# An attention block with a convolution for its queries: the first dense stage in another order, and the cast of later queries one slot later

## The chip, the core and the metric

The kernel runs on one core of a Trainium2 chip. The metric is the time of one execution in microseconds (us) on the device. TensorE is called PE, VectorE DVE, ScalarE ACT, GpSimd POOL and SyncE SP, as in the profile.

## The reference

`x` is [4, 384, 48, 48] in float32: 4 images, 384 channels, 2304 pixels each. Per image:

```
local  = depthwise 7x7 convolution of x, scaled and shifted per channel
qkv    = layernorm(x over channels) @ qkv_w.T + qkv_b      # 8 heads of 48
q      = q + layernorm(local)                              # the convolution goes to the queries
attn   = softmax(q @ k.T * 48**-0.5)                       # 2304 x 2304 per head
out    = x + (attn @ v) @ proj_w.T + proj_b
```

## The kernel before

**Tiles.** Channels lie on the 128 partitions in three chunks. The dense stage (values, keys, queries from the normed x) goes by six groups of 384 columns (8 rows of 48 pixels). The attention goes by query tiles: 4 images x 5 tiles t of 8, 10, 10, 10 and 10 rows (384 or 480 columns). Each tile has 12 slots (four pairs of heads x three batches of keys). A slot is `score_batch` (36 matmuls, L1099; one exp on ACT per two banks, L1107) and `weigh_batch` (24 matmuls, L1114), 9.1 us of PE at 480 columns and 7.4 at 384.

**Order.** PE, DVE, ACT and SP run in the order in which the program is written (a manual schedule). POOL does so only up to `loads.close()`; from there a scheduler places its instructions. Each instruction waits on semaphores for what it reads.

**Convolution.** It runs on DVE, one instruction per tap and chunk (L337; 147 for a tile), for the next tile while PE works at this one. In the first dense stage the taps are placed by hand with `convolve_first(n)`; after that `plan()` deals them out in proportion to a table of free DVE time at each point (slots: `spare`; dense stages of later images: `spare_at_keys`, points ("kv", t, g, h)) and to the due time of each tile. What the first stage has made beyond tile 0's 147 taps is `made`, where the plan starts. Tile 1's first chunk is convolved on PE (`products`, L410).

**Norms.** The class `Norm` takes the mean over channels by a matmul with a matrix of constants. `mean_by_chunk` uses three matmuls, one for each chunk (L688, the line of `project`). `sum_squares` (two DVE adds, L560 and L561) and `mean_in_place` (one matmul, L593) do the same with DVE's adds. Then `centre` (L603), `squares` (ACT, L550), `root` (ACT, L611 to L613), `newton` (DVE, L625 and L626), `scale` (L683).

**First dense stage** (image 0, lines 1157 to 1268): group 0's x comes from the convolution's slab; weights are loaded into `staged[2]` (values), `staged[1]` (keys) and `staged[0]` (queries) and scaled by the norm's gain on ACT (L899, L906, L907). `shift_rows` (L862) and `columns` (L888) give the share of the norm's beta in the biases, which `key_bias` and `query_bias` (L910 to L916, DVE) add. `from_x` is a generator: each `next` (two in `both`) issues matmuls of values, keys or queries of a group and their evictions; `lows_out` writes the low parts of the keys (L798). `convolve_first`, the norm of the next group and these steps are interleaved by hand. SP issues, in order: the vectors, slab(0, 0) in two parts, the three weights, x of groups 1 to 5 (four DMAs each), the output weights `w_o`, and later `copies_in` (L358) for the shifted rows that `products` reads. POOL loads the slab of tile 1, which `conv_ops(0)` issues with its first tap.

**Queries.** `local_end` and `query_end` (L936, L948) make a tile's queries from the normed convolution and q. Each pair of heads is split in a high part (`high_queries`: cast on ACT, L962) and a low part (`low_queries`: subtraction on DVE, L967, and six DMAs on SP, L972 and L974, that stack rows). The scores of a pair read all of them. For the first pair of the next tile this happens in the slots of this tile: in image 0 and at t = 0 with the full norm ("early"), from t = 5 on with the short norm ("following", `few_...`, slots `first` = 5 and `second` = 8). `jobs` are ACT instructions that `weigh_batch` issues behind the exps of its slot. `query_end(t, True)` puts the cast between its first and second DVE instruction.

Of the kernel before, what the change touches and what calls it, by code (L numbers as in the profile page):

```python
# [10 lines left out]
F32 = mybir.dt.float32  # L11
# [5 lines left out]
P = 128  # L17
# [31 lines left out]
def unshifted_pass(  # L49
# [16 lines left out]
    nc = tc.nc  # L66
    B, C, N = x.shape
    W = 48
    H = N // W
    CC = C // P  # L70
    G = RG * W
    NG = N // G
# [7 lines left out]
    NT = B * NA  # L80
# [31 lines left out]
    def load_packed(dst, src, queue=nc.sync):  # L112
        for p0, piece in segments(src):
            queue.dma_start(out=dst[p0 : p0 + piece.shape[0]], in_=piece)
# [5 lines left out]
    def place_x(b, g):  # L120
        xn[b, g] = whole[:, :, g * G : (g + 1) * G]
        return xn[b, g]

    def load_x(b, g, queue=nc.gpsimd):
        load_packed(place_x(b, g), x[b, :, g * G : (g + 1) * G], queue)

    slabs = {}

    def load_slab(b, g, parts=1, queue=nc.gpsimd):
        first, end = max(0, row_of[g] - PAD), min(H, row_of[g + 1] + PAD)  # L130
        t = work.tile([P, CC, GM + 2 * PAD * W], F32, tag="slab", name=f"slab{b}_{g}")

        edges = (first, row_of[g + 1], end) if parts == 2 else (first, end)
        for a, e in zip(edges, edges[1:]):
            load_packed(t[:, :, (a - first) * W : (e - first) * W], x[b, :, a * W : e * W], queue)
        slabs[b, g] = (t, first, end)

# [58 lines left out]
                    )  # L196

    load_by_pair(of_ln, ln_pair, (nc.scalar, nc.gpsimd))
    load_slab(0, 0, 2, nc.sync)
    place_x(0, 0)  # L200
    nc.gpsimd.tensor_scalar_add(inv, norms[:, 3], BN_EPS)
    nc.gpsimd.tensor_tensor(inv, inv, neg_half, ALU.pow)
# [26 lines left out]
    def pack():  # L229
# [23 lines left out]
        work.tile([P, CC, GM], F32, tag="qs", name="copies", bufs=5).rearrange("p c n -> p (c n)")  # L253
        for _ in range(2)
    ]
    staged = [
        work.tile([P, CC, GM], F32, tag="qs", name="staged", bufs=5)[:, :, :C] for _ in range(3)
    ]
    load_packed(staged[2], qkv_wT[:, 2 * C :])
    load_packed(staged[1], qkv_wT[:, C : 2 * C])  # L260
    load_packed(staged[0], qkv_wT[:, 0:C])
    for g in range(1, NG):
        load_x(0, g, nc.sync)
    load_by_pair(qk_vec, qk_b, (nc.gpsimd, nc.gpsimd))
    with nc.allow_non_contiguous_dma(reason="a few vectors, once"):
        load_packed(vbp, v_b.rearrange("o c -> c o"), nc.gpsimd)
    nc.gpsimd.dma_start(out=pb, in_=proj_b)
    load_packed(w_o, proj_wT)
    loads.close()


# [33 lines left out]

    def conv_ops(t):
        b, g = divmod(t, NA)
        if t + 1 < NT:
            load_slab(*divmod(t + 1, NA))
        slab, first, end = slabs[b, g]  # L310
        if t == 0:
            begin_sums(0)
            begin_sums(1)
        while soon:
            soon.popleft()()
        acc = accs[t]

        order = [(tap, c) for tap in taps for c in range(CC)]
        if t == 1:
            order = [o for o in order if o[1]]  # L320
        for i, (tap, c) in enumerate(order):
            if i == len(order) - AHEAD and t + 1 < NT:
                if t:
                    begin_sums(t + 1)
                soon.append(lambda: first_taps(t + 1))
            part = window(slab, acc[:, c, :], g, first, end, c, tap)
            if not part:
                continue
            src, dst = part
            weight = cw[:, c, tap : tap + 1]  # L330
            if tap == taps[0]:
                if t == 0:
                    nc.vector.tensor_scalar(
                        dst, src, weight, shift[:, c : c + 1], ALU.mult, ALU.add
                    )
            else:
                nc.vector.scalar_tensor_tensor(dst, src, weight, dst, ALU.mult, ALU.add)  # L337
            if t == 0 or tap != taps[0]:
                yield
# [11 lines left out]
    def copies_in():  # L351

        slab, first, end = slabs[0, 1]
        slab = slab[:, 0].rearrange("p (h w) -> p h w", w=W)
        for q, rows in enumerate(quarters):
            for i, to in enumerate(quarters):
                n = min(rows_kept, end - first - i)
                nc.sync.dma_start(out=copy_of(q)[to, 0:n], in_=slab[rows, i : i + n])  # L358
# [104 lines left out]
    def spare_at_keys(b, g, h):  # L463
        time = 4.6 - {0: 0.6, 2: 0.7, 3: 1.4, 4: 1.2}.get(h, 0.0)
        if g < later(b):
            time -= {0: 2.3, 2: 2.2, 4: 2.3}.get(h, 0.0)
        if 0 < g <= later(b):
            time -= {1: 0.4, 3: 2.6}.get(h, 0.0)
        return time - {
            (1, 1): 1.0, (2, 1): 1.4, (4, 0): 2.3, (4, 2): 2.2, (4, 4): 2.3, (5, 0): 0.4,  # L470
            (5, 1): 4.5, (5, 2): 0.6, (5, 3): 1.5, (5, 4): 3.0,
        }.get((g, h), 0.0)

    points, room = [("start",)], [FIRST_ROOM]
# [278 lines left out]
    def keep_stack(b, i):  # L753
        at = slice(i * third, (i + 1) * third)
        nc.gpsimd.dma_start(out=wide[b, 0][:, :, at], in_=stacks[b, 0, i].bitcast(F32))
# [81 lines left out]
    def both(making):  # L837
        next(making)
        next(making)
        while soon:  # L840
            soon.popleft()()

    def lows_out(n):
        for _ in range(n):
            lows.popleft()()
# [72 lines left out]
    def output_bias():  # L918

        m = two_banks()[:, 0, 0:CC]  # L920
        for co in range(CC):
            project(
                m[:, co : co + 1],
                lambda c: w_o[:, c, co * P : (co + 1) * P],
                lambda c: vbp[:, c, :],
            )
        added = const.tile([P, CC], F32, tag="inv", name="added")
        nc.scalar.copy(added, m)
        return added
# [4 lines left out]
    def local_end(t, rs):  # L934
        acc = accs[t]
        nc.vector.scalar_tensor_tensor(acc, acc, -1.0, rs, ALU.mult, ALU.mult)  # L936
# [21 lines left out]
    def high_queries(t, p):  # L958
        qs = work.tile([P, 3, GM], HALF, tag="qs", name=f"qs{t}_{p}", bufs=5)
        qs = qs[:, :, : columns_of(t)]  # L960
        stacked[t, p] = qs
        nc.scalar.copy(qs[:, 0, :], query_of(t, p))  # L962
# [184 lines left out]
    def convolve_first(n):  # L1147
        nonlocal n_first
        n_first += n
        for _ in range(n):  # L1150
            next(stream)
# [28 lines left out]
    both(making)  # L1180
    shift_rows()
    rows_out()
    copies_in()
    spread_out()
    next(making)
    for c in range(CC):
# [2 lines left out]
    convolve_first(10)  # L1189
    norm = Norm(xn[0, 1])  # L1190
    norm.mean_by_chunk(norm.src, bank)
    convolve_first(18)
    key_bias(m)
    convolve_first(3)
    query_bias(m)
# [1 line left out]
    norm.centre()  # L1197
    norm.squares()
    both(making)
    convolve_first(2)  # L1200
    norm.mean_by_chunk(norm.buf)
    norm.root()
    both(making)
    convolve_first(4)
    lows_out(3)
    norm.scale(norm.newton())
    both(making)
    convolve_first(7)
    norm = Norm(xn[0, 2])
    norm.sum()  # L1210
    for g in range(1, NG):

        last = g == NG - 1
        making = from_x(0, g)
        both(making)
        if last:
            added = output_bias()
        else:
            norm.mean_in_place()
            convolve_first(6)  # L1220
        if g in (3, 5):
            keep_stack(0, g // 2 - 1)
        norm.centre()
        norm.squares()
        if last:
            convolve_first(6)
        both(making)
        if last:
            norm.mean_by_chunk(norm.buf)
        else:  # L1230
            if g == 1:
                taps_out()
            if g == 2:
                products()
                convolve_first(24)
            convolve_first(5)
            norm.sum_squares()
            both(making)
            norm.mean_in_place()
        norm.root()  # L1240
        if last:
            convolve_first(9)
            local_end(0, norm.newton())
            query_end(0, True)
            both(making)
            low_queries(0, 0, nc.scalar)
            convolve_first(2)
            lows_out(1)
            both(making)
            convolve_first(4)  # L1250
            both(making)
            continue
        lows_out(1)
        both(making)
        convolve_first(6)
        lows_out(2)
        norm.scale(norm.newton())
        both(making)
        if g == NG - 2:
            assert n_first >= each  # L1260
            norm = Norm(accs[0])
            norm.mean_by_chunk(norm.src)
        convolve_first(5)
        if g < NG - 2:
            norm = Norm(xn[0, g + 2])
            norm.sum()
    lows_out(2)
    nc.vector.tensor_add(pb, pb, added)
    made = n_first - each
# [3 lines left out]
    for t in range(NT):  # L1273
# [74 lines left out]
        for s in range(NSLOT):  # L1348
# [26 lines left out]
                norm_x.scale(norm_x.few_newton())  # L1375
            if following and s == second + 1:
                local_end(t + 1, norm.few_newton())
                query_end(t + 1, True)
            if coming and s == X_SLOTS[0] + 1:
                jobs.extend(norm_x.square_jobs())  # L1380
            if following and s == first + 1:
# [40 lines left out]
                low_queries(t, pair + 1)  # L1422
            if t and early and s == first + 1:
                norm.sum_squares()
            if following and s == second + 1:
                low_queries(t + 1, 0)
            if coming and s == X_SLOTS[0]:
                norm_x.few_centre()
# [579 lines left out]
```

## Time and profile before

| | before |
|---|---|
| runs, us | 2738.39, 2740.79, 2745.3 (median 2740.79) |
| profiled execution, us | 2736.99 |
| its span, us | 2735.1 |
| mean granted clock of PE | 0.999 |
| DVE busy, convolution alone (L337), us | 2313.1, 1657.9 |
| PE: weighing (L1114), scoring (L1099), us | 1166.2, 968.5 |
| first scores of tile 0 start at, us | 161.04 |
| scores of tile 1 start at, us | 255.66 |
| last projections start at, us | 2694 |

The span is that of the profiled execution; its time has 1.9 us around the span. In the views, a row names line, engine, operation, tile written <- tiles read, shapes and count; a bracket at its end gives the engine's idle time just before it and what ended it. A row of the timeline has the start and the length in us first, and joins several like instructions into one (x12). The view of waits lists, for an engine, the instruction that waited, what it waited for, the sum, how often and the longest, in us.

### The profile page before, as it was taken

The numbers are of one execution on the slowest core, as the hardware profiler recorded it, in microseconds if no ns is written. First come the engines' busy times: TensorE is split into PE (matmuls) and PEld (weight loads), VectorE is DVE, ScalarE is ACT, GpSimd is POOL, SyncE is SP. The second block draws the span as 40 slices with busy tenths as digits, with TensorE's granted clock in tenths as the row PEclk, the third lists the DMA queues.
The fourth block names the chain that finished last, engine by engine and source line by source line (L and its number), as shares of the span: only waits on it lengthen the run. The fifth ranks groups of instructions, "written<-read, shape, count | busy, mean of one in ns | idle before, by whom it ended". The sixth has DMA issues, their size and how long they took to land.

```text
span 2735.1 us, 46034 instructions
## 1 busy us (share of the span) xinstructions
PE 2715.1 (99%) x16442; PEld 1536.5 (56%) x16442; DVE 2313.1 (85%) x4036; ACT 1671.0 (61%) x2317; POOL 599.5 (22%) x1073
## 2 busy tenths in 40 slices
PE   8999999999999999999999999999999999999999
PEld 5565555555566555555555655555555665555555
DVE  7999999989998899988889899889788898986212
ACT  4356777777325767777622677777752377766762
POOL 4541101102452111011155210111225511110110
PEclk9999999999999999999999999999999999999999
DMA  8354535446456545354555553545536545444442
GB/s 164 85 153 129 143 112 138 126 128 179 107 146 162 133 124 147 112 156 117 150 138 135 166 152 104 143 127 144 144 111 159 153 134 135 136 134 130 141 150 68
DMA packets 160480, 370.46 MB, mean 135 GB/s; under 512 B 58673, under 2 KB 107857, under 8 KB 160241
## 3 DMA queue, kind: packets, MB, share of 16 engines
q0 software_dynamic: 71232, 278.45, 36.1%
q1 hardware_dynamic: 83696, 78.92, 12.6%
q10 hardware_dynamic: 5312, 10.06, 1.1%
q8 instruction: 132, 2.16, 0.3%
q14 instruction: 108, 0.88, 0.1%
HBM read 258.14 MB, written 64.14 MB: 118 GB/s over the span
## 4 chain that ended last, share of the span: by engine, by line
PE 89%; DVE 8%; DMA 2%; ACT 1%; SPq 0%; issue 0%; POOL 0%; DVEq 0%; ACTq 0%
PE o L1114 37%; PE r L1099 31%; PE r L688 20%; DVE acc L337 6%; DMA xn<-in_x_dram 1%; DMA rd<-den 0%; PE r L410 0%; DMA qs<-qs 0%; DMA slab<-in_x_dram 0%; SPq L974 0%; DVE acc L936 0%; DVE xn L948 0%; DMA staged<-in_qkv_wT_dram 0%; PE r L587 0%; DVE ao L1010 0%
## 5 line engine op out<-in xcount | busy, mean ns | idle before, releaser
L337 DVE SCALAR_TENSOR_TENSOR acc<-slab,vec,acc 128x470 f32<-128x470 f32 (+10 forms) x2832 | 1657.9, 656 | 4.2 <-ACT acc L300 4.2
L1107 ACT ACTIVATE pt<-r 128x960 f32<-128x960 f32 (+1 forms) x1440 | 1248.5, 943 | 246.1 <-PE o L1114 151.0
L1114 PE MATMUL o<-pt,v 128*64 128x480 f32 (+1 forms) x5760 | 1166.2, 554 | 0.4 <-ACT pt L1107 0.4
L1099 PE MATMUL r<-qs,ks 64*128 64x480 f32 (+1 forms) x8640 | 968.5, 373 | 3.1 <-DMA qs<-qs 1.2
L1099 PEld LDWEIGHTS r<-qs,ks 64*128 64x128 f32 x8640 | 785.0, 184 | 268.1 <-issue 173.2
L1114 PEld LDWEIGHTS o<-pt,v 128*64 128x64 f32 x5760 | 392.7, 137 | 659.7 <-issue 566.7
L760 POOL DMA_DIRECT2D ks<-wide x220 | 159.6, 726 | 1350.6 <-PE r L1099 1282.4
L688 PE MATMUL r<-xn,w_qk 128*128 128x384 f32 x864 | 284.2, 486 | 0.0
L991 ACT COPY o<-o 113x480 f32<-113x480 f32 (+1 forms) x160 | 87.1, 544 | 279.0 <-PE o L1114 278.5
L688 PEld LDWEIGHTS r<-xn,w_qk 128*128 128x128 f32 x864 | 164.1, 190 | 114.6 <-issue 0.7
L688 PE MATMUL r<-w_v,xn 128*128 128x384 f32 x432 | 146.9, 492 | 2.8 <-ACT w_v L899 2.5
L782 ACT COPY v<-r 128x384 f32<-128x384 f32 x72 | 32.1, 481 | 186.5 <-PE r L688 186.5
L1010 DVE TENSOR_TENSOR ao<-ao,o 113x480 f32<-113x480 f32 (+1 forms) x120 | 75.7, 631 | 71.6 <-ACT o L991 71.6
L688 PEld LDWEIGHTS r<-w_v,xn 128*128 128x128 f32 x432 | 82.2, 192 | 62.8 <-issue 4.1
L745 POOL DMA_DIRECT2D wide<-k x144 | 72.0, 502 | 100.4 <-ACT k L795 76.5
L967 DVE TENSOR_TENSOR qs<-xn,qs 128x480 fp32r<-128x480 f32 (+1 forms) x60 | 37.9, 632 | 60.1 <-ACT qs L962 60.1
L688 PE MATMUL r<-af,w_o 128*128 128x384 f32 (+1 forms) x270 | 85.2, 470 | 0.0
L1010 DVE TENSOR_TENSOR aot<-aot,o 113x480 f32<-113x480 f32 (+1 forms) x40 | 25.3, 632 | 62.7 <-ACT o L991 62.6
L1001 ACT COPY ao<-o 113x480 f32<-113x480 f32 (+1 forms) x60 | 32.6, 543 | 68.7 <-PE o L1114 68.7
L795 ACT ACTIVATE k<-r,qkb 128x384 fp32r<-128x384 f32 x72 | 39.3, 580 | 53.5 <-PE r L688 39.1
L812 ACT ACTIVATE xn<-r,qkb 128x384 f32<-128x384 f32 x72 | 39.9, 577 | 51.3 <-PE r L688 50.1
L1080 DVE SCALAR_TENSOR_TENSOR xr<-r,pb,xr 128x384 f32<-128x384 f32 (+2 forms) x72 | 41.9, 611 | 34.0 <-PE r L688 25.2
(147 smaller groups left out, 1358.6 us busy)
## 6 DMA issues: line engine op xcount, KB each, us to landing
ks<-wide POOLq DMA_DIRECT2D x220, 768.0 KB, 5.1
qs<-qs SPq DMA_DIRECT2D x352, 60.0 KB
slab<-in_x_dram POOLq DMA_DIRECT2D x24, 432.0 KB, 7.1
wide<-k POOLq DMA_DIRECT2D x96, 96.0 KB, 2.2
wide<-ks POOLq DMA_DIRECT2D x12, 768.0 KB, 4.9
xr<-in_x_dram POOLq DMA_DIRECT2D x16, 576.0 KB, 5.8
rb<-rden SPq DMA_DIRECT2D x32, 270.0 KB
held<-ao POOLq DMA_DIRECT2D x12, 720.0 KB, 3.9
```

Of the source, the lines that this page charges most:

```text
L337: nc.vector.scalar_tensor_tensor(dst, src, weight, dst, ALU.mult, ALU.add)
L688: nc.tensor.matmul(dst, lhsT=weights(c), rhs=src(c), start=c == 0, stop=c == CC - 1)
L745: nc.gpsimd.dma_start(out=last[16 * u : 16 * u + 16, 0], in_=k[r : r + 16, 0])
L760: queue.dma_start(out=place_keys(b, p, i), in_=wide[b, p][:, :, at])
L795: nc.scalar.activation(k[:, 0, :], r[:, :G], AF.Identity, bias=bias)
L812: nc.scalar.activation(src[:, i, :], q[:, :G], AF.Identity, bias=qkb[:, 0, i : i + 1])
L991: nc.scalar.copy(part[0 : 64 + HA], sums[0 : 64 + HA, 0, :n])
L1010: nc.vector.tensor_add(dst, dst, part[0 : 64 + HA])
L1080: nc.vector.scalar_tensor_tensor(xr[:, co, :], m, pb[:, co : co + 1], xr[:, co, :], ALU.add, ALU.add)
L1099: nc.tensor.matmul(r[:, j, :n], lhsT=ks[rows, w, at], rhs=qs[rows, m, :], start=i == 0, stop=i == 2,)
L1107: nc.scalar.activation(pt, r[:, :, :n], AF.Exp, scale=SCALE)
L1114: nc.tensor.matmul(sums[halves[j], 0, : columns_of(t)], lhsT=values[t // NA, kb // NB][:, first : first + 64], rhs=pt[:, j, :], start=i == ...
```

## The change

Five edits, all in the order of work; the arithmetic of the result is the same.

1. **Value weights first.** `load_slab` takes a function to call between its two parts; the DMAs of `staged[2]` go between the two parts of slab(0, 0) on SP. The staging tiles are allocated before the others.
2. **Loads.** x of group 1 is loaded alone, x of groups 2 and 3 and of 4 and 5 as pairs (8 DMAs fewer on SP). `w_o` goes from the end of SP's loads to POOL, written behind the norm's root in group 0; slab(0, 1) is written there too, and no longer in `conv_ops(0)`. `copies_in` is issued later.
3. **Key bias sooner**: 9 instead of 18 steps of `convolve_first` stand ahead of it.
4. **Chunk sums behind a norm.** The mean of squares of group 1 and of the convolution of tile 0 are taken by `sum_squares` and `mean_in_place` instead of `mean_by_chunk`. The taps of the first stage are placed anew; `made` goes from 32 to 21. The last group is written by itself behind the loop.
5. **Later casts.** For a "following" tile the cast comes as a job in slot `second + 2` = 10, `low_queries` at the end of slot 10 instead of 9; `query_end` no longer holds the cast. Two entries of the table `spare_at_keys` change.

```diff
-    def load_slab(b, g, parts=1, queue=nc.gpsimd):
+    def load_slab(b, g, parts=1, queue=nc.gpsimd, between=None):
...
         for a, e in zip(edges, edges[1:]):
+            if a != first and between is not None:
+                between()
...
-    load_slab(0, 0, 2, nc.sync)
+    load_slab(0, 0, 2, nc.sync, lambda: load_packed(staged[2], qkv_wT[:, 2 * C :]))
...
-    load_packed(staged[2], qkv_wT[:, 2 * C :])
     load_packed(staged[1], qkv_wT[:, C : 2 * C])
     load_packed(staged[0], qkv_wT[:, 0:C])
-    for g in range(1, NG):
-        load_x(0, g, nc.sync)
+    load_x(0, 1, nc.sync)
+    for g in range(2, NG, 2):
+        place_x(0, g)
+        place_x(0, g + 1)
+        at = slice(g * G, (g + 2) * G)
+        load_packed(whole[:, :, at], x[0, :, at], nc.sync)
...
-    load_packed(w_o, proj_wT)
     loads.close()
...
-        if t + 1 < NT:
+        if 0 < t < NT - 1:
             load_slab(*divmod(t + 1, NA))
...
-            (5, 1): 4.5, (5, 2): 0.6, (5, 3): 1.5, (5, 4): 3.0,
+            (5, 1): 4.5, (5, 2): 0.6, (5, 4): 1.5,
...
-    convolve_first(18)
+    convolve_first(9)
     key_bias(m)
...
     both(making)
-    convolve_first(2)
-    norm.mean_by_chunk(norm.buf)
+    convolve_first(3)
+    norm.sum_squares()
+    norm.mean_in_place()
     norm.root()
+    load_slab(0, 1)
+    load_packed(w_o, proj_wT, nc.gpsimd)
     both(making)
...
+    making = from_x(0, NG - 1)
+    both(making)
+    added = output_bias()
+    keep_stack(0, 1)
+    norm.centre()
+    norm.squares()
+    convolve_first(3)
+    norm.sum_squares()
+    norm.mean_in_place()
+    norm.root()
+    both(making)
+    convolve_first(6)
+    local_end(0, norm.newton())
+    query_end(0, True)
+    both(making)
+    low_queries(0, 0, nc.scalar)
+    convolve_first(4)
+    lows_out(1)
+    both(making)
+    convolve_first(8)
+    both(making)
     lows_out(2)
...
             if following and s == second + 1:
                 local_end(t + 1, norm.few_newton())
-                query_end(t + 1, True)
+                query_end(t + 1)
+            if following and s == second + 2:
+                jobs.append(lambda: high_queries(t + 1, 0))
...
-            if following and s == second + 1:
+            if following and s == second + 2:
                 low_queries(t + 1, 0)
```

In the loop over the middle groups (1 to 4) the conv's steps move too: 8 behind `mean_in_place` (6 before), 5, 33 or 9 ahead of `sum_squares` (5, 29 and 5 before), 4 behind `lows_out(1)` (6 before), and in group 4 five steps ahead of the mean of tile 0's convolution, where they stood behind it; `norm.scale` comes ahead of `lows_out(2)`.

## The prediction

> **What bounds the kernel now.** I read the page first, then the waits of PE, then the timelines of the stretches that the diff touches. The page, busy time and chain:
>
> ```profile
> PE 2715.1 (99%) x16442; PEld 1536.5 (56%) x16442; DVE 2313.1 (85%) x4036; ACT 1671.0 (61%) x2317; POOL 599.5 (22%) x1073
> ...
> PE o L1114 37%; PE r L1099 31%; PE r L688 20%; DVE acc L337 6%; DMA xn<-in_x_dram 1%; DMA rd<-den 0%; PE r L410 0%; DMA qs<-qs 0%; DMA slab<-in_x_dram 0%; SPq L974 0%; DVE acc L936 0%; DVE xn L948 0%; DMA staged<-in_qkv_wT_dram 0%; PE r L587 0%; DVE ao L1010 0%
> ```
>
> PE is busy in 99% of 2735.1 us: the time is PE's work plus its waits. The view of PE's waits (us in total, times, longest) shows how little is left to gain:
>
> ```profile
> PE r L593 <- DVE sq L561: 2.7, 1, 2.7
> PE r L688 <- ACT w_v L899: 2.5, 2, 2.0
> PE r L688 <- ACT sq L550: 2.5, 1, 2.5
> PE r L1157 <- POOL one L166: 1.8, 1, 1.8
> PE r L1099 <- DMA qs<-qs: 1.2, 2, 0.9
> PE r L1099 <- issue: 1.1, 1, 1.1
> ```
>
> All its waits make some 15 us, the largest in the first dense stage (0 to 161 us). Taking every one away could not give 1%. A new wait at a place that recurs could cost more. So I walk the first stage, then the casts, which come twelve times.
>
> **First stage, up to the second group's norm.** PE's timeline from 14 to 42 us (start, length, what, wait before it):
>
> ```profile
> 16.26 0.91 PE L688 MATMUL r<-w_v,xn 128*128 128x384 f32 x2 [1.98 <-ACT w_v L899]
> 17.70 5.19 PE L688 MATMUL r<-w_v,xn 128*128 128x384 f32 x10 [0.53 <-ACT w_v L899]
> 22.81 2.11 PE L862 MATMUL r<-staged,of_ln 128*1 128x384 f32 x18
> ...
> 30.82 2.17 PE L688 MATMUL r<-xn,mean_w 128*128 128x384 f32 x6 [0.57 <-DMA xn<-in_x_dram]
> 32.83 4.03 PE L688 MATMUL r<-xn,w_qk 128*128 128x384 f32 x12
> 39.34 2.20 PE L688 MATMUL r<-sq,mean_w 128*128 128x384 f32 x6 [2.48 <-ACT sq L550]
> ```
>
> Value weights first take away the two waits (2.5 us). PE then meets other gates sooner: the last key and query weights (staged[1] lands at 18.5, used from 22.81) and x of group 1 (its last DMA landed at 30.70, PE waited 0.57). So this part alone buys nothing that group 1's x does not allow; call X its landing. Six value matmuls between 17.7 and 22 us took 6.0 us where 3.9 is their time at full clock: the granted clock was 0.50 from 18 to 21 us, after that idling. Whether that stretch goes or moves, it lies ahead of X.
>
> w_o, 590 KB, was last on SP, behind x. Read in the schedule of the changed kernel, its first DMA (221 KB) stands at the head of POOL's queue and the others behind slab(0,1), whose DMAs were issued at 4.3 and 15.2 to 17.4 us. It now competes with x of group 1. Before, 140 to 211 GB/s were moved in each ten us up to 40 us, with the 16 engines' share at 1.08 between 15 and 30 us: they were full. If w_o takes nothing from x, X stays at 30.7, and 28.5 is the bound if x gains too. If all 590 KB go first, at 180 GB/s that is 3.3 us: 34.0. Before, some 0.5 MB of later groups had already come by 30.7, so SP loses only part: I take 31.7, near the row.
>
> The Trainium skill speaks against this move: "Trainium Kernel Development and Optimization", section Key Constraints, says that DMAs of SP's, ACT's and POOL's queues all run on the same 16 engines and interleave, and that several queues save only the time to issue. The full share agrees; by this rule alone X would be the 34.0 above, by the row of x's landing 30.7.
>
> Key bias sooner: before, the centring of group 1 (L603) began at 36.73, behind 27 taps (0.51 us each) that kept the key bias back to 34.83. Now nine taps fewer stand ahead, so the centring C waits for X: mean 1.94 (six records of 0.32) and bias, C = X + 2.4 = 34.1. From C to the next group's mean of squares (63.17 before, "L593") three more taps (1.5) and two adds (1.06) must run on DVE; less the idle they fill this path is 28.8 instead of 26.4. So that mean moves by (C - 36.73) + 2.35: -0.3 at X = 31.7, -1.3 at 30.7, +2.0 at 34.
>
> **First stage, the rest.** Chunk sums behind a norm: a mean by chunk is three matmul instructions of 0.645 us; one remains. Two norms x 2 x 0.645 = 2.6 us less on PE. DVE gets two adds of 1.06. From that mean to the first scores took 97.87 us (63.17 to 161.04); without the second mean and a wait of 0.33 PE's own work is 95.5. But two waits come. In group 4, the mean of the conv's result now stands behind five taps: DVE is ready 7.85 after the norm's mean, PE at 6.45: 1.4. In the last group the mean follows output_bias at once, and needs a copy (0.16), squares (1.17 on ACT), the sum (1.06) and 0.14: 2.7. Sum 99.6, +1.75. The dense stage ends **1.5** later (-1.7 at 28.5, +0.5 at 30.7, +3.8 at 34). The POOL and SP moves otherwise (keep_stack, copies, eight SP DMAs fewer) lie beside PE work; the copies are used only at 78.8 us.
>
> Eleven taps fewer are done in the first stage, and the planner gives them to later slots. In tile 0 DVE had no idle time from 157 to 240 us and PE already waited 0.52 at the norm (237.12). DVE now starts 1.0 later against PE and has two taps more ahead (1.25): **+2.3** (0 to 3.3). At tiles 1 to 4 DVE idles over 5 us before each query: nothing is carried on.
>
> **Later casts.** For the 12 tiles from the fifth on that are not first of an image, `low_queries` moves from the end of slot 9 to the end of slot 10, behind slot 10's taps on DVE. Its six DMAs on SP (3.7 us to issue) must land before the next tile's first scores. The same order exists already at tile 1; DVE there, and then PE:
>
> ```profile
> 248.58 0.65 DVE L967 TENSOR_TENSOR qs<-xn,qs 128x480 fp32r<-128x480 f32 x1
> 249.15 5.47 DVE L337 SCALAR_TENSOR_TENSOR acc<-slab,vec,acc 128x450 f32<-128x450 f32 x9
> ```
> ```profile
> 255.66 0.92 PE L1099 MATMUL r<-qs,ks 64*128 64x480 f32 x5
> 257.49 1.79 PE L1099 MATMUL r<-qs,ks 64*128 64x480 f32 x14 [0.91 <-DMA qs<-qs]
> ```
>
> From the subtraction to PE going on are 8.9 us, with a wait. At tiles 2 and 3 the gap was 8.44 without a wait, at tile 4 9.85 with 0.2; a 384-column tile needed 5.4 to 6.4 (835.34 to 841). I call it the need: 5.4 to 9.85, taken as 8.0, nearest the rows of 480 columns. Now the tiles of 480 columns, DVE and PE around tile 7:
>
> ```profile
> 1024.90 4.27 DVE L337 SCALAR_TENSOR_TENSOR acc<-slab,vec,acc 128x450 f32<-128x450 f32 x7
> 1029.09 0.65 DVE L967 TENSOR_TENSOR qs<-xn,qs 128x480 fp32r<-128x480 f32 x1
> 1029.65 12.42 DVE L337 SCALAR_TENSOR_TENSOR acc<-slab,vec,acc 128x450 f32<-128x450 f32 x20
> ```
> ```profile
> 1036.62 3.79 PE L1114 MATMUL o<-pt,v 128*64 128x480 f32 x18
> 1040.34 2.85 PE L1099 MATMUL r<-qs,ks 64*128 64x480 f32 x24
> ```
>
> The slack is 1040.34 - 1029.09 = 11.25. Behind 13 taps more (0.62 each, 8.2 with what else is there) 3.05 are left, 4.95 short of the need. In the same way (slack, delay, wait): tile 6: 11.2, 6.2, 3.0; tile 8: 14.4, 7.7, 1.3; tile 11: 11.9, 6.2, 2.3; tile 16: 12.4, 5.7, 1.3; tiles 9, 12 to 14 and 17 to 19 have 17.4 to 19.7 and wait for nothing. Sum **+12.9**; 17.4 with a need of 8.9, 4.8 with 6.2, 2.8 with 5.4. In each tile DVE waits for something that PE's end of the tile before sets (rd, L1036), so one wait does not pay for the next.
>
> What the later cast gives: ACT no longer stands before an exp waiting for the query:
>
> ```profile
> 1022.58 0.59 ACT L962 CAST qs<-xn 128x480 fp32r<-128x480 f32 x1 [3.39 <-DVE xn L948]
> ```
>
> There PE's scores took 5.07 instead of 4.10 us: 0.97 back. But it lies in tile 6, ahead of tile 7's scores, which then come sooner by as much and wait longer: **0** net. Planner: with its table, five taps more (two at one point, three at the next; 3.2 us) stand ahead of the last residual sum (L1080 at 839.18) before tile 5 and hold its PSUM; of them some 1.3 fall into a wait that PE had there anyway (1.07 at 840.72): **+1.9** (0 to 2.4; at tiles 10 and 15 DVE idles 3.5 and 2.5 there and hides it).
>
> Sum: 1.5 + 2.3 + 12.9 + 0 + 1.9 = +18.6. Against the profiled execution (2736.99; span 2735.1) that is 2755.6. The median of the runs, 2740.79, lies 3.8 above it: **2759**.
>
> **The rivals.**
> *The DMAs land sooner* (the other side: not slower). Mechanism: at slot 11 little else is on SP, the need is the 5.4 of the 384-column tile. Place: the starts of tiles 6, 7, 8, 11, 16. Price 2.8 instead of 12.9; with X at 30.7 the sum is 0.5 + 2.3 + 2.8 + 1.9 = +7.5, 2748. It decides from a need of about 5.5 down. For it: 5.4 was seen. Against: six issues alone take 3.7 and every 480-column row is at 8.4 or above.
> *x late and the need long.* w_o's bytes all ahead of x (X = 34, +3.8) and a need of 8.9 to 9.85 (17.4 to 22): 3.8 + 2.3 + 1.9 + 20 = +28, 2769. For it: the DMA share above 1.0 up to 30 us.
> *It does what its words say.* PE loses 2.6 us of matmuls and the first waits, DVE hides the sums, and the later casts only remove ACT's block: -2 to -5, 2737. Against: DVE has no gap in 157 to 240 us, and five boundaries have under 15 us of slack.
>
> **How the numbers follow.** Forecast 0.55, sooner landing 0.20, late x 0.13, as its words say 0.12. 0.3% (8.2 us) is about what a measurement of this kernel can tell from no change. Faster needs under 2732.6: part of the last case and what no row shows, 0.10. Same: most of the second case and the rest of the last, 0.24. Slower: 0.66. The range takes in the lower bounds (-1.7 + 2.3 + 2.8 + 0, 2744) with a little of the last case, and the late x: 2741 to 2770.
>
> **What would show it.** In the changed profile: waits of L1099's successor on DMA qs<-qs at the starts of tiles 6, 7, 8, 11, 16, of 1 to 5 us; x of group 1 landing at 31 to 32 and PE's mean there; new waits before the mean near 138 and 146 us; the first scores at 162 to 163; a wait of some 2.8 at the norm near 239. I am wrong if PE has no qs waits at those boundaries, or if the first scores start before 160.

## The result and the profile after

The changed kernel takes 2770.43 us (median of 4 runs, 2768.09 to 2779.42) against 2741.28 (2738.39 to 2745.3): 1.0111 times as long, 95% interval 1.0085 to 1.0137, or 29 us more. Forecast were 18 more, 2759, and at most 2770. The profiled execution is the slowest of the four, 2779.42 us (span 2777.6), 42.4 above the profiled one of before; its mean granted clock is 0.990, that of the other three 0.993 or 0.994, of before 0.999.

The page of the changed kernel, busy time and chain:

```profile
PE 2732.5 (98%) x16434; PEld 1547.8 (56%) x16434; DVE 2317.0 (83%) x4040; ACT 1672.4 (60%) x2317; POOL 602.4 (22%) x1077
...
PE 79%; DVE 11%; DMA 5%; issue 2%; ACT 1%; SPq 0%; POOL 0%; DVEq 0%; ACTq 0%; POOLq 0%
```

PE has 8 records less to do and is busy 17 us longer: the same matmuls took more time. Its waits (total, times, longest, in us):

```profile
PE r L1103 <- DMA qs<-qs: 13.8, 7, 3.9
PE r L597 <- DVE sq L565: 7.6, 2, 5.0
PE r L692 <- DVE acc L341: 2.8, 1, 2.8
PE r L1161 <- POOL mean_w L165: 2.8, 1, 2.8
PE r L692 <- issue: 2.4, 1, 2.4
PE r L692 <- DMA xn<-in_x_dram: 2.4, 1, 2.4
```

All idle time of PE, short gaps included, is 45.1 us in place of 20.0 (span less busy time): 25.1 more, where the span grew by 42.5. The other 17.4 are PE's own busy time, and the clock makes them. PE's timeline of the first stage (start, length, wait in the bracket) shows it in the lengths:

```profile
10.54 3.80 PE L692 MATMUL r<-slab,mean_w 128*128 128x128 f32 x18 [2.37 <-issue]
...
23.95 3.94 PE L866 MATMUL r<-staged,of_ln 128*1 128x384 f32 x18 [1.97 <-DMA pb<-in_proj_b_dram]
...
35.57 4.18 PE L692 MATMUL r<-xn,mean_w 128*128 128x384 f32 x6 [2.36 <-DMA xn<-in_x_dram]
...
69.18 1.62 PE L597 MATMUL r<-sq,mean_w 128*128 128x384 f32 x2 [5.00 <-DVE sq L565]
149.05 2.97 PE L692 MATMUL r<-acc,mean_w 128*128 128x384 f32 x6 [2.82 <-DVE acc L341]
161.31 1.62 PE L597 MATMUL r<-sq,mean_w 128*128 128x384 f32 x2 [2.59 <-DVE sq L565]
```

Compare with before: the same six mean matmuls took 2.17 us there and 4.18 here, the 18 of the beta rows 2.11 and 3.94, two records of a mean 0.88 and 1.62. Each slow row stands behind a bracket of about 2 us or more. Not every such bracket has a slow row behind it. In the kernel before, this one has none:

```profile
63.17 0.88 PE L593 MATMUL r<-sq,mean_w 128*128 128x384 f32 x2 [2.68 <-DVE sq L561]
```

The granted clock gives the same: the profiled execution has 11 stretches at 0.50 while PE works, each 3.4 us long or 6.8, 51 us together; before it had one of 3.4. Half of that, less what lies in PE's idle time, is lost: PE is busy 17.4 us longer although the change takes 2.6 us of matmuls away, so the clock costs **some 20 of the 42 us** of this execution, and the waits the rest. It is the slowest of the four. By its clock (0.990, against 0.993 or 0.994 and 0.999 before), the other three lose some 12 of their 29 us in this way: an estimate in proportion, as only this execution has a trace.

Where the two profiled executions part (start of the first scores of a tile, us):

| start of | before | after | behind | half of the time at half clock so far, waits included, after |
|---|---|---|---|---|
| tile 0 | 161.04 | 178.69 | 17.7 | 15.4 |
| tile 1, second slot | 266.09 | 286.39 | 20.3 | 17.1 |
| tile 5, second slot | 848.28 | 874.10 | 25.8 | 18.8 |
| tile 6, second slot | 938.52 | 969.93 | 31.4 | 20.5 |
| tile 7 | 1040.34 | 1069.75 | 29.4 | 20.5 |
| tile 11 | 1595.11 | 1624.52 | 29.4 | 20.5 |
| tile 12 | 1704.05 | 1741.58 | 37.5 | 23.9 |
| tile 17 | 2367.73 | 2409.82 | 42.1 | 25.6 |

The first stage loses 17.7, the tiles behind it 24.4. (Before, the last column is 1.7 throughout.)

### The profile page after: what moved, and what is told of

It is laid out like the page before. It is cut to its first block, busy times and chain, and to the rows that moved or that the text cites. A ratio compares the mean times of both kernels' runs of the same rounds, so it can differ in the third digit from the quotient of the medians.

```text
span 2777.6 us, 46010 instructions
## 1 busy us (share of the span) xinstructions
PE 2732.5 (98%) x16434; PEld 1547.8 (56%) x16434; DVE 2317.0 (83%) x4040; ACT 1672.4 (60%) x2317; POOL 602.4 (22%) x1077
## 3 DMA queue, kind: packets, MB, share of 16 engines
q1 hardware_dynamic: 82352, 78.33, 12.6%
## 4 chain that ended last, share of the span: by engine, by line
PE 79%; DVE 11%; DMA 5%; issue 2%; ACT 1%; SPq 0%; POOL 0%; DVEq 0%; ACTq 0%; POOLq 0%
PE o L1118 36%; PE r L1103 30%; PE r L692 12%; DVE acc L341 7%; DMA four<-parts 1%; DMA qs<-qs 1%; DMA parts<-part 1%; DVE k L802 1%; DMA xn<-in_x_dram 1%; DMA staged<-in_qkv_wT_dram 0%; DVE xr L1084 0%; PE r L414 0%; DVE sq L565 0%; DVE xn L952 0%; DMA wide<-k 0%
## 5 line engine op out<-in xcount | busy, mean ns | idle before, releaser
L1103 PE MATMUL r<-qs,ks 64*128 64x480 f32 (+1 forms) x8640 | 976.7, 375 | 16.3 <-DMA qs<-qs 13.8
L816 ACT ACTIVATE xn<-r,qkb 128x384 f32<-128x384 f32 x72 | 40.0, 579 | 50.5 <-PE r L692 49.2
L692 PEld LDWEIGHTS r<-af,w_o 128*128 128x128 f32 x270 | 51.3, 190 | 31.9 <-DVE k L802 0.2
```

The costliest lines, as they stand in the source:

```text
L692: nc.tensor.matmul(dst, lhsT=weights(c), rhs=src(c), start=c == 0, stop=c == CC - 1)
L816: nc.scalar.activation(src[:, i, :], q[:, :G], AF.Identity, bias=qkb[:, 0, i : i + 1])
L1103: nc.tensor.matmul(r[:, j, :n], lhsT=ks[rows, w, at], rhs=qs[rows, m, :], start=i == 0, stop=i == 2,)
```

## The experiments

**Theory A**: idle stretches of PE of some 1.5 us and more are followed by stretches at half clock, so that a wait costs its length and 1.7 or 3.4 us more. (The bound did not hold as a rule: see the last section.) **Theory B**, the rival (and the way the prediction counted): a wait costs its length. Beside them stands which edit makes which wait. In brackets behind a median stand the median of the kernel before, measured beside it, the ratio and its 95% interval.

**e1: the first stage alone.** The last edit undone, table and all.

```diff
-                query_end(t + 1)
-            if following and s == second + 2:
-                jobs.append(lambda: high_queries(t + 1, 0))
+                query_end(t + 1, True)
-            if following and s == second + 2:
+            if following and s == second + 1:
                 low_queries(t + 1, 0)
```

> The changed kernel with its last edit undone: casts and low parts of the later queries where they were, and the old table of the planner. In the changed profile the tiles from 5 on lose 21.4 us (from 20.65 behind at the end of tile 4 to 42.09 behind at tile 17). Theory A (every wait of PE longer than about 1.5 us is followed by stretches of 3.4 us at half clock, so it costs its length and 1.7 to 3.4 more): all of that goes, waits and stretches at tiles 5, 6, 11, 15 and 16; against the changed kernel -17 to -22 us, some 2750. Theory B (the waits alone cost): the qs and residual waits of these tiles sum to 13.5 us, so -13 us, some 2757. If the first stage alone made the loss, nothing changes.

Measured: 2754.3 us (2740.47; 1.0045, 1.0028 to 1.0062), 16 below the changed kernel, between the two numbers: the time does not decide between the theories. In its profile no tile from 6 on loses anything; tile 5's part of the path still holds a wait of 3.0 (for an eviction on ACT, L816) and one stretch, so that loss is not the last edit's alone. So the first stage, with this wait, costs some 14 us and the casts some 16 here.

**e2: the casts alone**, the same edit in the kernel before.

> The kernel before with the last edit alone (later casts and the new table). Theory A: waits at the starts of tiles 5, 6, 11 and 16, each with a half-clock stretch behind it where it is longer than 1.5 us: +17 to +22 us, some 2760, mean clock below 0.998. Theory B (waits alone): +13, some 2754, clock as before. The prediction's own sum for this part was +14.8 with waits at tiles 6, 7, 8, 11 and 16.

Measured: 2759.49 (2740.47; 1.0064, 1.0047 to 1.0081), +19.0, and mean clock 0.994 to 0.996: theory A. (The interval's lower end is +12.9, so it is the clock more than the time that rules out B.) The new waits are at tiles 5, 6, 11 and 16, as expected; the stretches behind 5, 6 and 11 were 6.8, 3.4 and 10.2 us long. With e1 the parts sum to 14 + 19 = 33; together they made 29.

**e3: w_o back on SP.**

```diff
     nc.gpsimd.dma_start(out=pb, in_=proj_b)
+    load_packed(w_o, proj_wT)
     loads.close()
...
-    load_packed(w_o, proj_wT, nc.gpsimd)
```

> The changed kernel with the output weights back at the end of SP's loads. Theory A with w_o as the cause of the first stage's loss: slab and x of group 1 land 2 to 5 us sooner (x by about 31 instead of 35.4), PE's wait before that mean and the half clock behind it go, first scores at 162 to 168 instead of 178.7; -8 to -14 us, some 2758. Rival (the order of the other loads and the new tap places cost it): first scores stay at 175 or later, -3 us at most.

Measured: 2763.99 (2740.47; 1.0079, 1.0062 to 1.0096), 6.4 below the changed kernel; first scores at 171.98, 6.7 sooner. Both lie between what the two expectations said, so neither cause has the whole loss. The mean of group 1's x shows no wait any more. But 11 us of the first stage's loss stay: w_o is under half of it.

**e4 and e5: waits filled.** Matmuls that nobody reads stand where PE waits. They take away no wait, they keep PE busy in it.

```diff
             weigh_batch(t, s)
+            if s == NSLOT - 1 and t in FILL:
+                warm(FILL[t])
```

> The changed kernel with matmuls that nobody reads (a constant by the identity, 0.38 us each) put on PE behind the last slot of tiles 0, 5, 10 and 15: 4, 9, 14 and 5 of them, as long as the waits for qs there (1.6, 3.5, 5.3, 1.5 us). The waits are then filled with work, not removed: the next scores can start no sooner. Theory A: PE is not idle, the half-clock stretches behind these four places (1.7, 1.7, 3.4 and 1.7 us lost) go: -6 to -9 us, and the first slot of tiles 1, 6, 11 and 16 takes 9.1 us. Theory B: no gain, 0 to +2 us from filling too much.

Measured: 2771.28 (2740.47; 1.0111, 1.0094 to 1.0128): no gain, a miss for theory A by its total. The reason is in the profile: in this place one such matmul took 0.24 us, not 0.38, so 9 and 14 of them were too short; waits of 1.6 and 2.5 stayed at tiles 6 and 11, with their stretches. Where the fill was long enough (tiles 1 and 16) no stretch came, and from the end of the tile before to the second slot it took 10.7 instead of 12.6 and 10.9 instead of 12.5. e5 fills again by this size, and the first stage too.

> The changed kernel with matmuls that nobody reads put in each longer wait of PE: ahead of L866 (9), of the mean of group 1's x (11), of group 1's mean of squares (20), of the mean of the convolution (11) and of the last group's (10), and behind the last slot of tiles 0, 5, 10, 15 (6, 17, 24, 7). In the run before one such matmul took 0.24 us, so the fills are as long as the waits measured (2.0 to 2.9, 2.4, 5.0, 2.8, 2.6; 1.6, 3.5, 5.3, 1.5). Theory A (idle PE is followed by stretches at half clock, which cost 24 us in the changed profile): the stretches go at all filled places, first scores at 166 to 170 instead of 178.7, total 2748 to 2757. Theory B (the waits and the longer order alone cost): no gain, 2768 to 2775.

Measured: 2763.02 (2741.19; 1.0085, 1.0068 to 1.0102), its four runs within 2762.7 to 2764.6, clock 0.998 or 0.999. First scores at 167.0, 11.7 sooner than in the profile of the changed kernel. PE in stretches (window, its length, busy, count, granted clock, DMA share, GB/s), the changed kernel:

```profile
0.00:50.00 50.00, 40.51 (x174) 0.86 1.01 161
50.00:100.00 50.00, 45.00 (x214) 0.93 0.37 97
100.00:150.00 50.00, 47.18 (x147) 1.00 0.37 87
150.00:200.00 50.00, 47.41 (x254) 0.90 0.56 129
```

and with the waits filled:

```profile
0.00:50.00 50.00, 42.94 (x226) 1.00 1.00 166
50.00:100.00 50.00, 49.54 (x262) 1.00 0.40 104
100.00:150.00 50.00, 49.55 (x181) 1.00 0.43 101
150.00:200.00 50.00, 49.39 (x335) 1.00 0.59 146
```

0.86, 0.93 and 0.90 become 1.00. No edit made anything come sooner that the real work waits for; only PE was not idle. (x of group 1 did come sooner in this execution: PE read it at 33.63, in the changed kernel's it landed at 35.4. So up to 1.9 of the 11.7 may be that.) The median lies between the two expectations (2748 to 2757 and 2768 to 2775). Theory A holds in direction: 7 us of the median, 17 between the profiled executions (the slowest of four there, the fastest of four here), and the spread. Theory B's "no gain" falls. What is left, some 22 us, would be the waits themselves and fills that were too long, with one stretch of 6.8 us at tile 5, whose wait was not filled; it was not divided further.

**e6: w_o on POOL alone**, in the kernel before.

> The kernel before with the output weights on POOL alone. If their bytes ahead of slab and x make the loss of the first stage: group 0's first mean starts at 10 or later instead of 8.3, x of group 1 lands 3 to 5 us later than 30.7, first scores 4 to 9 us later than 161; +4 to +9 us, some 2747. If only the order of SP and the new tap places count: 0 to +1.

Measured: 2742.82 (2741.19; 1.0007, 0.9997 to 1.0016): not told from no change, a miss for the +4 to +9 by w_o's bytes. Its profile has the late x (the mean of group 1's x at 34.16 behind a wait of 2.7; before, 30.82), and first scores 4.2 later. Of that 4.2 not all need be w_o's: e2 and e8, whose first stage is unchanged, have their first scores 2.6 and 2.9 later than the kernel before. Part of the lateness falls into slack: the centring of group 1 waited for taps until 36.73 before and starts at 38.74 here, 2.0 later for an x 3.3 later.

**e7: the key bias sooner alone.**

```diff
-    convolve_first(18)
+    convolve_first(9)
     key_bias(m)
...
-    convolve_first(2)
+    convolve_first(11)
     norm.mean_by_chunk(norm.buf)
```

> The kernel before with the key bias sooner alone (9 steps of the convolution moved from ahead of it to behind the squares of group 1). By the prediction's own sum the centring of group 1 then starts 2.4 behind x's landing, at 33.1 instead of 36.7, and the dense stage ends up to 3.6 us sooner: -1 to -4 us, some 2738. If DVE's work and not this wait binds the stage, 0. If the mean of squares then meets a wait of PE that the moved steps cause, +1 to +4 with its half clock.

Measured: 2739.38 (2741.19; 1.0001, 0.9991 to 1.001): nothing. The centring of group 1 did start sooner (32.65 instead of 36.73), but the mean of squares that the prediction followed from there came at 62.77 instead of 63.17: the taps moved behind it are still ahead of that mean on DVE. Where x is not late, this edit alone buys no time.

**e8: the price of a wait.** ACT copies that nobody reads hold up one slot in each of eight tiles.

```diff
+            if s == 4 and t in DOSE:
+                jobs.extend([lambda: nc.scalar.copy(junk, ident[:, 0:16])] * DOSE[t])
             weigh_batch(t, s)
```

> The kernel before with small ACT copies that nobody reads behind the exps of slot 4 of eight tiles: 14, 19, 24, 30, 36, 42, 48 and 60 of them in tiles 2, 3, 7, 8, 12, 13, 17 and 18, some 0.19 us each (2.7 to 11 us). ACT then holds up PE for about that time less 2.4 us (the block of 3.4 in tile 6 of the kernel before cost PE 0.97). Theory A: from a PE wait of some 1.5 to 2 us on, a tile loses its wait and 1.7 or 3.4 us more, in a stretch at half clock behind it. Theory B: each tile loses its wait alone, and the clock stays at 1.00.

One run, 2790.61 us. PE's rows behind the waits, one for each of tiles 3, 7, 8, 12, 13, 17 and 18 (tile 2 has none):

```profile
530.96 2.66 PE L1099 MATMUL r<-qs,ks 64*128 64x480 f32 x18 [0.62 <-ACT o L991]
1096.49 2.65 PE L1099 MATMUL r<-qs,ks 64*128 64x480 f32 x18 [1.80 <-ACT o L991]
1209.36 3.97 PE L1099 MATMUL r<-qs,ks 64*128 64x480 f32 x18 [3.21 <-ACT o L991]
1771.72 3.69 PE L1099 MATMUL r<-qs,ks 64*128 64x480 f32 x18 [4.63 <-ACT o L991]
1888.41 3.97 PE L1099 MATMUL r<-qs,ks 64*128 64x480 f32 x18 [6.04 <-ACT o L991]
2453.88 3.92 PE L1099 MATMUL r<-qs,ks 64*128 64x480 f32 x18 [7.45 <-ACT o L991]
2575.06 3.97 PE L1099 MATMUL r<-qs,ks 64*128 64x480 f32 x18 [10.28 <-ACT o L991]
```

The same 18 records take 2.65 us behind waits of 0.62 and 1.80, and 3.7 to 4.0 behind the longer ones. The tiles took longer than in the kernel before by 1.37, 2.52, 6.16, 6.39, 9.11, 9.43 and 13.08 us: their wait and 0.7 up to 1.80, their wait and 1.8 to 3.1 from 3.21 on. The 0.7 stands there without half clock, so some 1.1 to 2.4 are the clock's. Theory A again, with a bound between 1.8 and 3.2 in this place. The price does not grow with the wait: at 7.45 and 10.28 part of the slow stretch lies in the wait itself.

**e9: means by chunk again**, in the changed kernel.

```diff
     convolve_first(3)
-    norm.sum_squares()
-    norm.mean_in_place()
+    norm.mean_by_chunk(norm.buf)
```

(twice; and the mean of tile 0's convolution ahead of five taps again)

> The changed kernel with the fourth edit undone: three matmuls instead of two adds and one matmul for the mean of squares of group 1 and of tile 0's convolution, and the mean of that convolution ahead of the five taps that stood before it (they move up to the products). If the sums behind a norm and the taps ahead of the means make the late waits of the first stage, the waits of 2.8 us (near 149) and 2.6 us (near 161) go with their stretches at half clock (1.7 and 3.4 us lost): first scores 8 to 10 us sooner than 178.7, total some 2761. If only w_o and the loads make the loss, first scores stay within 3 us of 178.

Measured: 2766.23 (2739.98; 1.0097, 1.0081 to 1.0112), 4.2 below the changed kernel, first scores 5.6 sooner. The wait near 149 is gone, that near 161 is 1.3 (for the squares), but still with a stretch of 6.8 us behind it: some half of what was expected.

**e11 and e12: what is left of the first stage.** e11 is e1 with w_o on SP and the means by chunk of e9. e12 also moves five taps of group 1 from ahead of the centring of group 2's x to behind the next mean.

> The changed kernel with w_o on SP, the casts as before and the means by chunk: what is left is value weights first, x in pairs, slab(0, 1) behind the norm, the key bias sooner and the tap places. If the loss is made by w_o, the sums and the casts, this lies within 4 us of the kernel before (2737 to 2745). If value weights first or the tap places cost by themselves, 2748 or more, with first scores at 168 or later.

Measured e11: 2745.99 (2739.98; 1.0023, 1.0014 to 1.0032), 6.0 above before: a miss by 1 us of the expected bound, and below the 2748 of the rival. A wait of 4.99 at 62.85 is still there, the one that the changed kernel has at 69.18, with 6.8 us at half clock.

> As e11, but five of the taps that stand ahead of the centring of group 2's x (15 before, 10 now) are moved behind that group's mean of squares. In e11 PE waited 4.99 us at that mean (62.85) and ran 6.8 us at half clock behind it. Theory A: five taps less (0.5 us each) make the wait 2.5 us and the half-clock stretch 3.4 us or none: the mean starts near 60.4, first scores 3 to 6 us sooner than 166.5, -3 to -5 us against e11 (some 2742). If the later taps then hold up the norm's end, a new wait at the next values and no gain.

```diff
-        convolve_first(8)
+        convolve_first(3 if g == 1 else 8)
         norm.centre()
...
-        convolve_first(4)
+        convolve_first(9 if g == 1 else 4)
```

Measured e12: 2743.39 (2739.95; 1.0015, 1.0006 to 1.0024), 2.6 below e11, just short of the expected 3 to 5, and the two intervals overlap: the profile says more than the time. The row of e11 and then that of e12:

```profile
62.85 1.62 PE L598 MATMUL r<-sq,mean_w 128*128 128x384 f32 x2 [4.99 <-DVE sq L566]
```
```profile
60.91 0.88 PE L598 MATMUL r<-sq,mean_w 128*128 128x384 f32 x2 [2.76 <-DVE sq L566]
```

Five taps less ahead, 2.2 us less of wait, and the stretch behind it is 3.4 instead of 6.8 us. So for this wait it is the taps on DVE ahead of the mean that PE waits for.

**e10: the kernel before, its own waits filled** (18 instead of 14 at the start, 8, 10 and 11 at three places).

> The kernel before with matmuls that nobody reads in its own waits: 18 instead of 14 at the start, 8 ahead of the first values, 10 and 11 ahead of the means of squares of groups 1 and 2. Theory A: the runs of the kernel before that have a mean clock of 0.997 (2740 to 2744) lose 2 to 5 us in stretches at half clock that the runs at 0.999 (2736.7 to 2739) do not have; filled, all runs lie at 0.999 and near 2737: -2 to -5 us of the median, and the spread of the runs shrinks. Theory B: 0, or +1 from filling too much.

Measured: 2738.07 (2739.98; 0.9991, 0.9982 to 1.0), clock 0.999 or 1.0 in all 11 runs. It is the fastest version of the study by its median, 1.9 us below the kernel before, at the edge of what can be told from no change. The spread did not shrink (5.8 us, 2735.3 to 2741.1; before 5.6), which theory A had expected it to.

## Why the prediction was wrong

The direction was right and the places mostly; the size failed, in both halves. By medians, the first stage with tile 0 was to cost 3.8 us (1.5 + 2.3) and cost 13.8 (e1, with tile 5's wait); casts and table were to cost 14.8 (12.9 + 1.9) and cost 19.0 alone (e2). By its steps:

- **"Six value matmuls ... took 6.0 us where 3.9 is their time at full clock ... Whether that stretch goes or moves, it lies ahead of X."** The row was read, and then no other wait in the sum was given such a stretch. This is the step that failed most: some 20 of 42 us in the profiled execution. e5 and e8 show that the stretch comes with the idle time: filled, it is gone; made, it comes. The profile before did not make that price certain: of its waits of 1.98, 2.48 and 2.68 us only the first has a stretch behind it.
- **X = 31.7.** x of group 1 landed at 35.4, past the bound of 34.0. With w_o on POOL (six profiles) the mean of group 1's x starts at 33.63 to 36.19, with w_o on SP (eight) at 29.27 to 32.80. The bare sharing rule that it cited would have been nearer than the value chosen. Group 0's first mean is late too (10.54 instead of 8.33), but that is not shown to be w_o's: it starts at 9.65 to 10.45 in six profiles with w_o on SP.
- **C = X + 2.4.** It was X + 4.8 (40.19): the mean ran at half clock (4.18 instead of 2.17).
- **From the mean of squares to the first scores, 99.6.** It was 109.5. The two new waits are where they were put (1.4 and 2.7 forecast, 2.82 and 2.59 measured); nearly all of the rest is half clock behind the three waits, in stretches of 6.8, 3.4 and 6.8 us. As far as its terms can be followed, the sum is also short by some 0.5 of its own: the four terms of the last wait make 2.5 and not 2.7, and the 95.5 takes the second mean out whole, where one of its three matmuls (0.65) stays.
- **+2.3 in tile 0.** 2.65 by the second slot of tile 1, but as a wait of 1.45 at the norm and one of 1.60 for qs with a stretch.
- **The boundaries, +12.9, and tile 5, +1.9.** From tile 5 on 21.4 were lost. The slack left at tiles 6, 11 and 16 was forecast well (5.0, 5.7, 6.7; measured 5.31, 6.00, 6.63). The need was mis-sized: 8.0 against 9.3, 12.9 and 9.05 from the subtraction to PE going on. Its two rows in which PE had waited gave 8.9 and 9.85; the 8.44 had no wait, so it bounds the need from above only. So the waits were longer, and each had its stretch. The chosen case was the right one against the rival of a 5.4 need. That the total is no further off is partly luck: tiles 6, 11 and 16 lost 17.3 (5.6, 8.1 and 3.5) where the sum had 6.6, and its 6.25 for tiles 7 and 8 never came. Tile 5's loss is not the table's alone either: e1, with the old table, waits 3.02 there, and e6 3.30.
- **"One wait does not pay for the next."** It does: tiles 7 and 8 had 4.95 and 1.3 in the sum and waited for nothing (8.82 and 10.58 of slack). In tile 6 rd came 11.5 us behind the second slot's start, before 19.7, and DVE stood still 2.17 instead of 8.59 us for it. Why the chain of rd came sooner was not tried.
- **ACT's block, 0 net.** Tile 6 gave back 2.0 and tile 7 did not wait: a gain of 2, not 0.

The boundary row of tile 11 shows both halves of the price, the waits and the slow scores behind them (31 in 5.41 us; 4.1 is the time of 36):

```profile
1628.85 1.17 PE L1103 MATMUL r<-qs,ks 64*128 64x480 f32 x4 [3.85 <-DMA qs<-qs]
1631.42 5.41 PE L1103 MATMUL r<-qs,ks 64*128 64x480 f32 x31 [1.40 <-DMA qs<-qs]
```

Of the gains, the two value waits are gone and bought nothing that shows, as forecast: the next gate took them. The 2.6 us of matmuls, which the sum had counted as a gain, were outweighed by the waits that came with them: e9, with those matmuls back and five taps behind the mean again, is 4.2 us faster. Open stays how the 14 us of the first stage divide: w_o gives back 6.4 and the means by chunk 4.2 when undone one at a time, and e11 leaves 6.0, which sums to 16.6.

## What to carry to other kernels

Where one engine is busy 99% of the time, a new wait of it is not priced by its length alone: look in the trace for a row behind an old wait whose matmuls take longer than elsewhere, and add that to the upper end of each new wait. It comes behind some waits and not behind others. A transfer moved to another queue is counted from the moment at which it is issued there, against everything then in flight. And before a step is moved one slot later, the slack is measured at the tightest place that it recurs at, with the longest need that the trace shows, not the middle one.

## What the runs showed of the hardware

The stretches at 0.50 come in lengths of 3.41 us and its multiples, whatever the wait before them (1.3 us in e9 to 10.3 in e8). The length of the wait alone does not decide whether one comes: waits of 1.50 and 1.60 us at tiles 16 and 1 of the changed kernel were followed by one, waits of 1.80 in e8, 2.68 in the kernel before and 3.17 in e7 were not.

What the traces do show is a grid. The starts of the changed kernel's eleven stretches lie 4, 3, 10, 24, 3, 34, 173, 27, 196 and 197 times 3.413 us apart, to 0.01 us, and in every other trace with more than one the starts lie on such a grid too. Cut into these windows from PE's first matmul to its last, the 14 traces have 43 at full clock in which PE was busy less than 40% of the time: 42 were followed by half clock. Of the 11008 with 82% or more none was, of the 114 between them 21. So a wait can be cheap when the grid cuts it in two. Here the 2.68 us of the kernel before fall into two windows, and the 5.00 us of the changed kernel fill one (window, length, PE's busy time and count, granted clock, DMA share, GB/s):

```profile
58.89:62.30 3.41, 1.61 (x5) 1.00 0.00 0
62.30:65.71 3.41, 2.54 (x8) 1.00 0.41 108
```
```profile
65.01:68.42 3.41, 0.00 (x0) 1.00 0.26 75
68.42:71.84 3.42, 2.66 (x4) 0.50 0.28 76
```

In the range between, busy time is not the whole answer. Of the 15 windows over 50% that were followed by half clock, seven hold matmuls of one column and the other eight scores, which stand in windows that were not followed by it too; what weighs there was not tried.

The Trainium skill, "TensorE: Matmul & The Clock Gate", Part 1, section "What's actually happening", has the frame for this: two states of PE's clock, half and full, chosen by activity in a window of 3.4 us that runs freely. The lengths and the grid agree with 3.41. It gives one idle window of about 3.4 us as what brings the slow state; by the measurement, which decides, 1.5 to 2.8 us were enough in seven places of the changed kernel, and a window need not be idle throughout.

The clock also goes with some of the scatter of the kernel before. Of 61 of its runs beside the experiments, 16 had a mean clock of 0.997 (median 2741.9 us), 16 of 0.998 (2740.2) and 27 of 0.999 (2739.2). It is not the main part of it: e10's runs all have 0.999 or 1.0 and still spread over 5.8 us.
